# Moving the layer norms' subtraction and multiplication from VectorE to GpSimd in a two-layer cross-attention block

## The chip, the cores and the metric

The kernel runs on one core of one Trainium2 chip. The metric is the device time of one execution in microseconds. Engines are named as the profile names them: PE (TensorE matmul), PEld (TensorE weight load), DVE (VectorE), ACT (ScalarE), POOL (GpSimd) and SP (SyncE, which here issues nearly all DMAs).

## The reference

Two transformer layers run on `x` of 4 x 512 x 320 floats with a context of 4 x 1601 x 192. Each layer has three blocks, and each block begins with a layer norm over the 320 features:

```python
def _ln(x, g, b):
    m = jnp.mean(x, axis=-1, keepdims=True)
    v = jnp.mean(jnp.square(x - m), axis=-1, keepdims=True)
    return (x - m) * jax.lax.rsqrt(v + EPS) * g + b
...
h1 = _ln(x, n1_g, n1_b)
x = _attn(h1, h1, q1, k1, v1, o1_w, o1_b, heads) + x        # 20 heads of 16
h2 = _ln(x, n2_g, n2_b)
x = _attn(h2, context, q2, k2, v2, o2_w, o2_b, heads) + x   # keys and values from the context
h3 = _ln(x, n3_g, n3_b)
proj = h3 @ ff_w1 + ff_b1
a, g = jnp.split(proj, 2, axis=-1)
return a * jax.nn.gelu(g, approximate=False) @ ff_w2 + ff_b2 + x
```

So there are 2 layers x 3 blocks x 4 batches = 24 norms, each over 512 rows, which lie as four tiles of 128 rows by 320 features.

## The kernel before

**Units.** The work is cut into 88 units in a fixed order. In each layer come 20 self-attention units (4 batches x 5 groups of 4 heads), then 20 cross-attention units in the same way, then 4 feed-forward units. An attention unit goes over its keys in chunks of 128: 4 chunks in self attention, 13 in cross attention. For each chunk PE makes the scores of four heads (`st`, line 1282), ACT takes the exponential into a buffer `pr` (line 1292), and PE multiplies with the values (`av`, line 1308). ACT copies the product out of PSUM (`vo`, line 1327) and POOL adds it to the running sum `o` (line 1328). The pool `prs` has nine buffers for `pr` and `vo`.

**The work laid beside it.** The row maxima that the softmax of a coming unit needs are made early. PE makes score products into PSUM banks (`sps`, line 1054) while the current unit runs, and DVE reduces each bank to a maximum (`pm` or `nmax`, line 1069). There are eight PSUM banks for everything, so a bank that DVE has not read yet holds PE up. At the end of that, `max_end` turns the maxima, and four DMAs on SP's queue bring them to the rows that the scores need (`nrows<-turned`, line 1133). After a unit, `oway<-o` (line 1152) sends the sums to DRAM, on SP's queue too.

**Rounds and chains.** While the program is written, a counter `clock["round"]` is stepped twice a chunk. All other work (projections, norms, values, divisions, context) stands in chains: `add(chain, cost, f, due, ready, soon)` appends a step, and `steps()` runs, after each round of products, those heads of chains whose conditions hold, the earliest due first, as the credit allows. A step with cost `LIGHT` also uses up one of the one or two lights of that call; a step with cost 0.0 does not. On each engine instructions run in the order written.

**A norm** is `add_norm(l, b, i, ...)`: `i` is 0 for self attention, 1 for cross attention, 2 for feed forward. `stats` takes mean and variance of each tile on DVE (lines 546 and 547), `root` finds the reciprocal square root by Newton steps, on POOL after the start (lines 513 and 520 to 523). Then there are two ways:

- Norms with `first` (self attention of layer 0, self attention of batches 2 and 3 in layer 1, cross attention of batch 0) use `plain`: per tile three DVE instructions (line 608) subtract the mean, multiply, and write `hturned` with a step of 4 or 3 elements. Then `turn` transposes on PE (`hps`, line 621) and ACT applies gain and bias (line 629).
- The others use `normalise` (one DVE instruction per tile, line 562, into `hn`, which has one buffer) and `blocks` (a DVE transpose of 32 x 32 blocks into `hturned`, line 568). Then DMAs on SP's queue bring the blocks into place (line 578), and POOL applies gain and bias (`affine`, line 595).

The norm of a batch runs while earlier units still compute; `until_normed` would force what is left of it when a unit needs it.

Of the kernel before, what the change touches and what calls it, by code (L numbers as in the profile page):

```python
# [24 lines left out]
NQ = N // P  # L25
# [50 lines left out]
def kernel(ctx: ExitStack, tc: tile.TileContext, x, context, ws, out):  # L76
# [18 lines left out]
    nc = tc.nc  # L95
# [199 lines left out]
    class Unit:  # L295


        def __init__(self, l, kind, b, g):
            self.l, self.kind, self.b, self.g = l, kind, b, g
            self.cross = kind == "cross"  # L300
            self.nkeys = S2 if self.cross else N
            self.nch = (self.nkeys + P - 1) // P

            self.moves = {"k": deque(), "q": deque()}
            self.moving = {"k": 0, "q": 0}
            self.open = 6 if self.cross else 3
            self.keyed = None
            self.when = None
            self.vmade = [0, 0]

            self.made = {"q": 0, "k": 0, "kv": 0}
            self.scored = 0
            self.valued = 0
            self.steps = 2 * self.nch if kind != "ff" else 2 * NHC + NQ
            self.before = None
            self.others = []
            self.early = False
            self.own = {}
            self.pairs = self.hT = self.kvT = None
# [63 lines left out]
    clock = {"round": 0, "credit": 0.0, "lights": 0, "tiles": None, "ff": False}  # L383
    ALIKE = ("project", "early", "proj", "values")
    LIGHT = 0.01
# [3 lines left out]
    start = {"on": True}  # L389
# [22 lines left out]
    def busy(engine, us, *tiles):  # L412
        expect[engine] = max([expect[engine]] + [bank_of[id(t)][3] + 0.05 for t in tiles]) + us
        for t in tiles:
            bank_free[bank_of[id(t)][0]] = expect[engine] + 0.09
# [12 lines left out]
    def add(chain, cost, f, due, ready=yes, soon=yes):  # L428
        chains[chain].append((cost if isinstance(cost, tuple) else (cost,), due, ready, soon, f))
# [74 lines left out]
    def guess_root(var):  # L504

        a, h, y, z = (two.tile([P, NQ], F32, tag=f"root{i}", name=f"root{i}") for i in range(4))
        nc.vector.tensor_scalar(a, var, EPS, None, ALU.add)
        nc.vector.tensor_scalar(
            z.bitcast(I32), a.bitcast(I32), 1, None, ALU.logical_shift_right
        )  # L510
        nc.vector.tensor_scalar(y.bitcast(I32), z.bitcast(I32), -1, 0x5F3759DF, ALU.mult, ALU.add)
        eng = nc.vector if start["on"] else nc.gpsimd
        eng.tensor_scalar(h, a, -0.5, None, ALU.mult)
        return h, y, z

    def better_root(h, y, z):


        eng = nc.vector if start["on"] else nc.gpsimd
        eng.tensor_tensor(z, y, y, ALU.mult)  # L520
        eng.tensor_tensor(z, z, h, ALU.mult)
        eng.tensor_scalar(z, z, 1.5, None, ALU.add)
        eng.tensor_tensor(y, y, z, ALU.mult)
# [13 lines left out]
    def add_norm(l, b, i, put, done, due):  # L537
        xb = xs[b]
        s = {}

        def stats(t):
            if t == 0:
                hn_used.append(b)
                s["mv"] = two.tile([P, NQ, 2], F32, tag="mv", name="mv")
            st = three.tile([P, 6], F32, tag="st6", name="st6")
            nc.vector.bn_stats(st, xb[:, t, :])
            nc.vector.bn_aggr(s["mv"][:, t, :], st)
            busy("dve", 0.65)

        def root(step):  # L550
            if step == 0:
                s["root"] = guess_root(s["mv"][:, :, 1])
                s["rstd"] = s["root"][1]
            for _ in range(step + 1):
                better_root(*s["root"])
            s["round"] = clock["round"]

        def normalise(t):
            if t == 0:
                s["turned"] = one.tile([P, DB, NQ, SLOT], F32, tag="hturned", name="hturned")  # L560
            s["hn"] = one.tile([P, D], F32, tag="hn", name="hn")
            nc.vector.tensor_scalar(
                s["hn"], xb[:, t, :], s["mv"][:, t, 0:1], s["rstd"][:, t : t + 1], ALU.subtract, ALU.mult,
            )
            busy("dve", 0.4)

        def blocks(t):
            nc.vector.transpose(s["turned"][:, :, t, :], s["hn"])
            busy("dve", 0.45)
            s["round"] = clock["round"]  # L570
# [32 lines left out]
        def plain(t):  # L603
            if t == 0:
                s["hn"] = one.tile([P, DB, NQ, SLOT], F32, tag="hturned", name="hturned").rearrange("p k t w -> p (k t w)")
            for k, at, n in HK:
                w = n // SLOT
                nc.vector.tensor_scalar(  # L608
                    s["hn"][:, t * D + at : t * D + at + n].rearrange("p (d k) -> p k d", k=w),
                    xb[:, t, at : at + n].rearrange("p (k d) -> p k d", k=w),  # L610
                    s["mv"][:, t, 0:1], s["rstd"][:, t : t + 1], ALU.subtract, ALU.mult,
                )
            busy("dve", 0.45)
            s["round"] = clock["round"]

        def turn(k, at, n):
# [19 lines left out]
        first = i == 0 and (l == 0 or b > 1) or i == 1 and b == 0  # L636
        ahead = 0 if first or i == 2 and b else EARLIER
        parts = [(0, 0, P, 0), (1, 4, 96, 0), (2, 7, 96, 0)]
        if i == 2:
            parts = [(0, 0, P, 0), (1, 4, P, 0), (2, 8, REST, 0), (2, 8, REST, REST)]  # L640
        left, moved = [len(parts) * P // SLOT], {}

        def later(n, key="round"):
            return lambda: clock["round"] >= s[key] + n

        def together(f):
            return [lambda ts=ts: [f(t) for t in ts] for ts in (((0, 1), (2, 3)) if i == 2 and b else ((0,), (1,), (2,), (3,)))]

        for t, f in enumerate(together(stats)):
            add(  # L650
                "norm", LIGHT, f, due - ahead - 22 + t,
                (lambda: stage[b] == 3 * l + i and not hn_used and b in loaded) if t == 0 else yes,
                (lambda: b == 0 or clock["round"] >= loaded[b] + 5) if t == 0 else yes,
            )
        for step in range(2):
            add(
                "norm", 0.0 if step else LIGHT, lambda step=step: root(step), due - ahead - 18 + step, yes,
                (lambda: clock["round"] > s["round"]) if step else yes,
            )
        if first:  # L660
            for t in range(NQ):
                add("norm", LIGHT, lambda t=t: plain(t), due - 13 + t, yes, yes if t else later(1))
            for k, at, n in HK:
                add(
                    "norm", 0.58, lambda k=k, at=at, n=n: turn(k, at, n), due - 6 + 2 * k,
                    may_overwrite if k == 0 else yes, later(1),
                )
            return
        for t, f in enumerate(together(lambda t: (normalise(t), blocks(t)))):
            add("norm", LIGHT, f, due - ahead - 13 + t, yes, yes if t else later(1))  # L670
        add("norm", 0.0, spread, due - ahead - 6, may_overwrite, later(1))

        def there(k):
# [106 lines left out]
    errands = deque()  # L780
# [333 lines left out]
    def max_end(u):  # L1114

        top, high, low = (u.nm[:, :, i, :] for i in range(3))
        nc.vector.tensor_reduce(
            high.bitcast(F32R), top.rearrange("p j (t o) -> p j t o", o=1), AX.X, ALU.max, negate=True
        )
        nc.vector.tensor_reduce(  # L1120
            low, u.nm[:, :, 0:2, :].rearrange("p j e t -> p j t e"), AX.X, ALU.add, negate=True
        )
        turned = two.tile([P, SLOT], F32, tag="turned", name="turned")

        nc.vector.transpose(turned.rearrange("p (j c) -> p j c", j=HG), u.nm[:, :, 1:3, :].rearrange("p j e t -> p j (e t)"))
        busy("dve", 0.6)
        slots = u.rows.bitcast(F32).rearrange("(g s) n -> s g n", s=DH)[0].rearrange("g (t r) -> g t r", t=NQ)

        def rows():
            for i in range(P // SLOT):  # L1130
                part = slice(i * SLOT, (i + 1) * SLOT)
                queue = (nc.sync, nc.scalar, nc.gpsimd, nc.sync)[i] if start["on"] else nc.sync
                queue.dma_start(out=slots[:, :, part], in_=turned[part, :])

        if u.cross and u.before.cross:
            errands.appendleft((clock["round"] + 1, yes, rows))
        else:
            rows()
# [133 lines left out]
    def main(u, give, nxt):  # L1272

        pr, raised = {}, {}

        def score(c, j):
            r = min(P, u.nkeys - c * P)
# [383 lines left out]
    first = units[0]  # L1661
# [69 lines left out]
```

## Time and profile before

| what | value |
|---|---|
| median of 3 runs | 2983.01 us (2982.85 to 2983.1) |
| profiled execution, own time | 2982.2 us |
| its span | 2980.4 us |
| mean granted PE clock | 0.994 |
| PE busy | 2874.4 us (96%) |
| DVE busy | 2119.6 us (71%) |
| ACT busy | 1889.8 us (63%) |
| POOL busy | 1193.4 us (40%) |

The page gives busy time by engine, the chain of work that ended last, and groups of instructions by line. A group's row has the engine, what it writes and reads, the shapes, the count, the busy sum, the mean duration in ns, and what the engine waited for before. Lines in these rows are those of the kernel before. The table of stretches gives, for each stretch of the span, the busy time of each engine with the number of instructions in brackets.

### The profile page before, as it was taken

To read this page: it belongs to the slowest core of one execution; us is meant where nothing else is said; L and a number is where in the kernel's file an instruction comes from. 1 tells how busy PE (TensorE), PEld (TensorE's weight loads), DVE (VectorE), ACT (ScalarE), POOL (GpSimd) and SP (SyncE) were. 2 spreads that over 40 slices of the span, in tenths; PEclk is the share of its full clock that TensorE was granted. 3 is DMA by queue.
4 is the path that set the end of the run, shared out by engine and by line. 5 is a ranking of instruction groups with operands and counts; after the bars stand their busy time and mean duration, and the time that the engine had idled before them with its cause. 6 is when DMAs were issued, how large, how long until landed. Compare 5 with 4: busy or idle time off the path is not lost.

```text
span 2980.4 us, 84363 instructions
## 1 busy us (share of the span) xinstructions
PE 2874.4 (96%) x35018; PEld 1511.5 (51%) x35018; DVE 2119.6 (71%) x4143; ACT 1889.8 (63%) x3746; POOL 1193.4 (40%) x1305
## 2 busy tenths in 40 slices
PE   8999999999999999999999899999999999999999
PEld 4455555555554555355554555555555555544555
DVE  7877888889889888323268778888898888873221
ACT  3766677877877878501137676778878778784000
POOL 3445344554544545211224443445445454451110
PEclk8999999999999999999999999999999999999999
DMA  4443233132132122200123342221221121222000
GB/s 105 104 125 97 71 80 95 49 89 60 48 91 68 39 56 61 83 17 14 38 60 73 92 100 68 61 61 48 62 64 46 49 71 42 55 56 77 23 22 14
DMA packets 186543, 188.70 MB, mean 63 GB/s; under 512 B 69668, under 2 KB 137264, under 8 KB 186160
## 3 DMA queue, kind: packets, MB, share of 16 engines
q1 hardware_dynamic: 185368, 182.11, 24.2%
q8 instruction: 276, 4.52, 0.6%
q10 hardware_dynamic: 760, 1.18, 0.2%
q14 instruction: 107, 0.88, 0.1%
q0 software_dynamic: 32, 0.00, 0.0%
HBM read 55.76 MB, written 29.36 MB: 29 GB/s over the span
## 4 chain that ended last, share of the span: by engine, by line
PE 79%; DVE 16%; ACT 1%; DMA 1%; issue 1%; POOL 1%; SPq 0%; ACTq 0%; POOLq 0%; DVEq 0%
PE av L1308 22%; PE st L1282 16%; PE fps L1393 9%; DVE pm L1069 8%; PE sps L1054 6%; PE yps L1500 6%; PE vps L1015 5%; DVE nmax L1069 4%; PE kps L951 4%; PE ops L1211 3%; PE qkps L886 3%; PE fps L1453 2%; PE qps L927 2%; PE sps L1081 1%; ACT pr L1292 1%; DVE hturned L608 1%
## 5 line engine op out<-in xcount | busy, mean ns | idle before, releaser
L1292 ACT ACTIVATE pr<-st 128x512 f32<-128x512 f32 (+1 forms) x2720 | 1405.1, 603 | 418.3 <-PE st L1282 382.4
L1069 DVE TENSOR_REDUCE pm<-sps 128x1 f32<-128x512 f32 x1920 | 1187.2, 682 | 136.3 <-PE sps L1054 125.8
L1328 POOL TENSOR_TENSOR o<-o,vo 128x512 f32<-128x512 f32 x576 | 740.3, 1285 | 1101.8 <-ACT vo L1327 1091.9
L1054 PE MATMUL sps<-kT,q 32*128 32x512 f32 x4800 | 866.5, 429 | 12.2 <-DMA q<-low 3.2
L1308 PE MATMUL av<-pr,vals 128*32 128x512 f32 (+1 forms) x5440 | 735.1, 606 | 72.3 <-DVE nmax L1069 18.5
L1282 PE MATMUL st<-q,kT 32*128 32x512 f32 (+1 forms) x5120 | 791.6, 421 | 1.3 <-DVE pm L1069 0.8
L1282 PEld LDWEIGHTS st<-q,kT 32*128 32x128 f32 (+1 forms) x5120 | 420.7, 180 | 289.7 <-issue 119.1
L1282 PE MATMUL st<-nrows,ones 32*128 32x512 f32 (+1 forms) x2720 | 542.5, 400 | 8.5 <-DMA nrows<-turned 8.5
L1054 PEld LDWEIGHTS sps<-kT,q 32*128 32x128 f32 x4800 | 423.4, 184 | 93.3 <-DVE nmax L1069 15.7
L1069 DVE TENSOR_REDUCE nmax<-sps 128x1 f32<-128x512 f32 x640 | 395.7, 681 | 85.9 <-PE sps L1054 83.0
L1327 ACT COPY vo<-av 128x512 f32<-128x512 f32 x576 | 352.4, 612 | 20.9 <-PE av L1308 19.9
L1464 ACT ACTIVATE gl<-fps,b 128x512 f32<-128x512 f32 x80 | 54.8, 687 | 414.3 <-PE fps L1453 303.0
L1308 PEld LDWEIGHTS av<-pr,vals 128*32 128x32 f32 (+1 forms) x5440 | 111.1, 108 | 347.2 <-DVE pm L1069 179.4
L1393 PE MATMUL fps<-hT,w 128*128 128x512 f32 x640 | 283.2, 597 | 0.0
L1282 PEld LDWEIGHTS st<-nrows,ones 32*128 32x128 f32 (+1 forms) x2720 | 246.7, 180 | 33.2 <-issue 7.2
L1465 DVE SCALAR_TENSOR_TENSOR hid<-fps,b,gl 128x512 f32<-128x512 f32 x80 | 59.7, 748 | 238.8 <-ACT gl L1464 236.7
L1393 PEld LDWEIGHTS fps<-hT,w 128*128 128x128 f32 x640 | 119.2, 190 | 155.1 <-issue 151.8
L1500 PE MATMUL yps<-w,hid 128*128 128x320 f32 x640 | 176.0, 435 | 0.1
L1500 PEld LDWEIGHTS yps<-w,hid 128*128 128x128 f32 x640 | 120.4, 190 | 56.5 <-ACT gl L1464 5.3
L1211 PEld LDWEIGHTS ops<-wo,aT 112*32 112x32 f32 (+1 forms) x3072 | 97.7, 110 | 64.1 <-issue 42.9
L1211 PE MATMUL ops<-wo,aT 112*32 112x160 f32 (+1 forms) x3072 | 125.9, 300 | 0.9 <-DVE pm L1069 0.7
L886 PE MATMUL qkps<-hT,wqk 96*32 96x256 f32 (+1 forms) x1920 | 121.3, 395 | 0.0
(89 smaller groups left out, 2340.2 us busy)
## 6 DMA issues: line engine op xcount, KB each, us to landing
kT<-stages SPq DMA_DIRECT2D x160, 200.2 KB
oway<-o SPq DMA_DIRECT2D x80, 256.0 KB
q<-high SPq DMA_DIRECT2D x160, 64.0 KB
q<-low SPq DMA_DIRECT2D x160, 64.0 KB
kT<-high SPq DMA_DIRECT2D x60, 128.0 KB
q<-high SPq DMA_DIRECT2D x60, 128.0 KB
kT<-low SPq DMA_DIRECT2D x57, 128.0 KB
aT<-oway SPq DMA_DIRECT2D x32, 224.0 KB
```

The costliest lines, as they stand in the source:

```text
L886: nc.tensor.matmul(ps[f : f + m, :w], lhsT=wqk[:n, k, f // GD, column : column + m], rhs=first.hT[:n, k, at : at + w], start=(k == 0), sto ...
L1015: nc.tensor.matmul(ps[f : f + m, :w], lhsT=u.kvT[:n, k, at + f : at + f + m], rhs=wv[:n, k, h0 * DH : h1 * DH], start=(k == 0), stop=(k == ...
L1054: nc.tensor.matmul(ps, lhsT=u.q[j * SLOT : (j + 1) * SLOT, e, t * P : (t + 1) * P], rhs=u.kT[j * SLOT : (j + 1) * SLOT, u.k0 + s * 512 : u ...
L1069: nc.vector.tensor_reduce(to[:, j : j + 1], ps, AX.X, ALU.max)
L1211: nc.tensor.matmul(ps[f : f + m, : D // 2], lhsT=aT[:n, k, f * NQ + t * SLOT : f * NQ + t * SLOT + m], rhs=wo[:n, k, cols], start=(k == 0) ...
L1282: nc.tensor.matmul(own[0][:r, :], lhsT=ones[rows, :r] if e == 2 else u.keys(rows, c), rhs=u.rows[rows, :] if e == 2 else u.q[rows, e, :], ...
L1292: nc.scalar.activation(p[:r], own[0][:r], AF.Exp)
L1308: nc.tensor.matmul(ps[j * SLOT : (j + 1) * SLOT, :], lhsT=columns_of[:r, head : head + SLOT], rhs=pr.pop((c, j))[:r, :], start=True, stop= ...
L1327: nc.scalar.copy(vo, ps)
L1328: nc.gpsimd.tensor_tensor(u.o, u.o, vo, ALU.add)
L1393: nc.tensor.matmul(ps, lhsT=w1[:, k, i * FF + c * P : i * FF + (c + 1) * P], rhs=natural(u.hT[:, k]), start=start, stop=stop,)
L1500: nc.tensor.matmul(ps[:, :D], lhsT=hid[c][:, t * P : (t + 1) * P], rhs=w2[:, c, :], start=(c == 0), stop=(c == NHC - 1),)
```

## The change

The subtraction and multiplication of a norm go from DVE to POOL in three places: in `plain` whenever the kernel is past its start, and in `normalise` unless the norm is `alone`, that is self attention (`i == 0`) or feed forward of batches 1 to 3. So it moves `normalise` of cross attention in batches 1 to 3 and of feed forward in batch 0, and `plain` of all its norms but the first two, which are run at the start. The model of engine times that the planner keeps (`busy("dve", ...)`) is told of DVE work only where DVE still does it. The moved steps cost 0.0 and no light.

The order in time is set anew around them. `first` norms past the start begin four rounds sooner (`sooner`), their tiles are at least one round apart, and the PE transposes follow four rounds after the last tile instead of one. In the other moved norms, `normalise` of a tile and its `blocks` are now steps of their own, at least two rounds apart, with due times three rounds apart from tile to tile.

The last edit runs, at the start of a cross unit's `main`, the four row DMAs of that unit if they still stand in `errands`.

```diff
@@ add_norm
+        alone = i == 2 and b > 0 or i == 0
...
-            nc.vector.tensor_scalar(
+            (nc.vector if alone else nc.gpsimd).tensor_scalar(
                 s["hn"], xb[:, t, :], s["mv"][:, t, 0:1], s["rstd"][:, t : t + 1], ALU.subtract, ALU.mult,
             )
-            busy("dve", 0.4)
+            if alone:
+                busy("dve", 0.4)
+            s["round"] = clock["round"]
...
-                nc.vector.tensor_scalar(
+                (nc.vector if start["on"] else nc.gpsimd).tensor_scalar(
                     s["hn"][:, t * D + at : t * D + at + n].rearrange("p (d k) -> p k d", k=w),
...
-            busy("dve", 0.45)
+            if start["on"]:
+                busy("dve", 0.45)
...
+        sooner = 4 if first and not start["on"] else 0
...
-                "norm", LIGHT, f, due - ahead - 22 + t,
+                "norm", LIGHT, f, due - ahead - 22 - sooner + t,
...
-                "norm", 0.0 if step else LIGHT, lambda step=step: root(step), due - ahead - 18 + step, yes,
+                "norm", 0.0 if step else LIGHT, lambda step=step: root(step), due - ahead - 18 - sooner + step, yes,
...
-                add("norm", LIGHT, lambda t=t: plain(t), due - 13 + t, yes, yes if t else later(1))
+                add("norm", LIGHT if start["on"] else 0.0, lambda t=t: plain(t), due - 13 - sooner + t, yes, later(1))
...
-                    may_overwrite if k == 0 else yes, later(1),
+                    may_overwrite if k == 0 else yes, later(1 if k or start["on"] else 4),
...
-        for t, f in enumerate(together(lambda t: (normalise(t), blocks(t)))):
-            add("norm", LIGHT, f, due - ahead - 13 + t, yes, yes if t else later(1))
+        if alone:
+            for t, f in enumerate(together(lambda t: (normalise(t), blocks(t)))):
+                add("norm", LIGHT, f, due - ahead - 13 + t, yes, yes if t else later(1))
+        else:
+            for t in range(NQ):
+                add("norm", 0.0, lambda t=t: normalise(t), due - ahead - 17 + 3 * t, yes, later(1))
+                add("norm", LIGHT, lambda t=t: blocks(t), due - ahead - 15 + 3 * t, yes, later(2))
@@ max_end
         if u.cross and u.before.cross:
+            u.rows_of = rows
             errands.appendleft((clock["round"] + 1, yes, rows))
@@ main
+        for todo in [e for e in errands if e[2] is u.rows_of]:
+            errands.remove(todo)
+            todo[2]()
```

More of the change, by code (lines that the diff above doesn't have):

```diff
@@ L300, in __init__ @@
             self.cross = kind == "cross"
+            self.rows_of = None
             self.nkeys = S2 if self.cross else N
```

## The prediction

> **What bounds the kernel now.** I read the page's engine table first, then the chain that ended last, then the rows of the norm, then tables of stretches around the norms.
>
> ```profile
> span 2980.4 us, 84363 instructions
> PE 2874.4 (96%) x35018; PEld 1511.5 (51%) x35018; DVE 2119.6 (71%) x4143; ACT 1889.8 (63%) x3746; POOL 1193.4 (40%) x1305
> ...
> PE 79%; DVE 16%; ACT 1%; DMA 1%; issue 1%; POOL 1%; SPq 0%; ACTq 0%; POOLq 0%; DVEq 0%
> ```
>
> PE is busy for 96% of the span, so PE's work is the floor, and what can be won is time in which PE waits: 2980.4 - 2874.4 = 106 us idle, plus whatever waiting hides inside modelled matmul ends. The chain says who makes PE wait: 16% of it runs over DVE, nearly nothing over POOL. POOL has 60% of the span free. So a DVE instruction that stands ahead of the maxima can cost time, and the same instruction on POOL is at first sight free. The question is how much of the moved work stands where PE waits. One stretch of self attention, as the chain in order of time, shows it:
>
> ```profile
> by line: DVE nmax L1069 45.7%; DVE hturned L608 29.5%; PE av L1308 13.2%; PE qkps L886 8.1%; PE st L1282 4.1%; issue 0.6%; PE sps L1054 0.4%
> ...
> 99.11 2.48 DVE nmax L1069 x4
> 101.60 2.34 DVE hturned L608 x6
> 103.94 0.58 DVE nmax L1069
> ```
>
> Two tiles of `plain` (six instructions, 2.34 us) stand in DVE's queue between the maxima; PE's next products wait until DVE has read the banks. That is the best case for the change. The next rows are what is moved and what it could cost on POOL.
>
> ```profile
> L562 DVE TENSOR_SCALAR hn<-x,mv,root 128x320 f32<-128x320 f32 x64 | 41.9, 654 | 9.2 <-POOL root L523 8.1
> L608 DVE TENSOR_SCALAR hturned<-x,mv,root 128x96 f32<-128x96 f32 x64 | 21.6, 393 | 0.0
> L595 POOL TENSOR_SCALAR hT<-hT,lng,lnb 128x512 f32<-128x512 f32 x32 | 24.7, 772 | 127.6 <-DMA hT<-hturned 116.0 <-PE ops L1211 11.6
> L522 POOL TENSOR_SCALAR root<-root 128x4 f32<-128x4 f32 x66 | 14.8, 224 | 5.8
> ...
> L507 DVE TENSOR_SCALAR root<-mv x24: 157/170/1068, 5.8 to 2866.0; 128x4 f32<-128x4 f32 x24
> ```
>
> **What leaves DVE.** Six norms lose `plain` (24 tiles, 72 instructions) and eight lose `normalise` (32 instructions). The busy time of just those, by stretches that hold them and no others, and of the transposes that stay beside the 32:
>
> ```profile
> 60.00:360.00 300.00, 15.60 (x36) 1.00 0.40 102
> 1530.00:1750.00 220.00, 14.79 (x36) 0.97 0.36 88
> ...
> sum 1340.00, DVE 27.13; mean DVE 13.57
> ...
> sum 1340.00, DVE 16.36; mean DVE 8.18
> ```
>
> The first two rows are line 608 in the two self stages (15.60 + 14.79 = 30.4 us), the third is line 562 in cross attention (27.1 us), the last is line 568 there (16.4 us). So 57.5 us leave DVE, but most of a DVE microsecond is not a PE microsecond. I size that by PE's idle time in the stretches with a moved norm, against stretches of equal length right behind them. Columns after the length: PE, PEld, DVE, ACT, POOL busy. First self attention, with `plain`, then the stretches behind:
>
> ```profile
> 98.00:114.00 16.00, 13.32 (x194) 6.76 (x184) 15.13 (x32) 11.19 (x23) 7.27 (x13) 1.00 0.40 94
> ...
> 1575.00:1593.00 18.00, 13.87 (x180) 7.12 (x180) 14.45 (x30) 11.26 (x23) 7.44 (x15) 0.91 0.22 51
> 1655.00:1673.00 18.00, 12.64 (x164) 5.96 (x160) 13.12 (x29) 10.03 (x21) 7.62 (x15) 0.91 0.44 116
> ...
> sum 94.00, PE 75.85 PEld 38.91 DVE 84.41 ACT 61.90 POOL 43.27; mean PE 12.64 PEld 6.48 DVE 14.07 ACT 10.32 POOL 7.21
> ```
> ```profile
> sum 94.00, PE 91.97 PEld 50.36 DVE 67.31 ACT 73.33 POOL 36.83; mean PE 15.33 PEld 8.39 DVE 11.22 ACT 12.22 POOL 6.14
> ```
>
> With `plain`, DVE is busy for 84.41 of 94 us and PE idles 94 - 75.85 = 18.2 us; behind it PE idles 2.0 us. Two of the six stretches (1575 and 1655) hold 4.13 + 5.36 = 9.5 of that, with DVE far from full, so something other than DVE's load waits there. The other four idle (18.2 - 9.5) / 4 = 2.2 us each. I count all six at 2.2 and take the usual idle off: 6 x 2.2 - 2.0 = **11 us** from `plain`. Counting the two in full would give 16.
>
> Cross attention in the same way, eight stretches with `normalise` and eight behind:
>
> ```profile
> 702.00:720.00 18.00, 16.45 (x244) 8.11 (x240) 17.77 (x31) 13.47 (x27) 8.31 (x15) 1.00 0.51 132
> ...
> sum 122.00, PE 111.01 PEld 53.99 DVE 118.04 ACT 88.98 POOL 60.23; mean PE 13.88 PEld 6.75 DVE 14.75 ACT 11.12 POOL 7.53
> ```
> ```profile
> 720.00:738.00 18.00, 17.71 (x280) 10.23 (x284) 14.85 (x32) 13.35 (x28) 7.05 (x6) 1.00 0.16 34
> ...
> sum 122.00, PE 119.91 PEld 68.84 DVE 97.26 ACT 91.84 POOL 41.84; mean PE 14.99 PEld 8.60 DVE 12.16 ACT 11.48 POOL 5.23
> ```
>
> DVE is nearly full here (118.04 of 122), PE idles 11.0 us against 2.1 us, an excess of 8.9 us. The transposes stay, so I give the change the moved share of the norm's DVE time: 27.1 / (27.1 + 16.4) = 62% of 8.9 = **5.5 us**. All of it, if the transposes alone fit into DVE's slack, would be 8.9.
>
> Why `normalise` is as dear as 654 ns in the mean is seen in its spread and in the order of time:
>
> ```profile
> L562 DVE TENSOR_SCALAR hn<-x,mv,root x64: 426/446/1507, 496.7 to 2876.6; 128x320 f32<-128x320 f32 x64
> ```
> ```profile
> 704.64 1.29 POOL L1328 TENSOR_TENSOR o<-o,vo 128x512 f32<-128x512 f32 x1
> 704.84 1.27 DVE L562 TENSOR_SCALAR hn<-x,mv,root 128x320 f32<-128x320 f32 x1
> 706.15 0.51 DVE L568 STREAM_TRANSPOSE hturned<-hn 128x320 f32<-128x320 f32 x1
> 708.41 1.29 POOL L1328 TENSOR_TENSOR o<-o,vo 128x512 f32<-128x512 f32 x1 [2.48 <-ACT vo L1327]
> 708.95 0.93 DVE L562 TENSOR_SCALAR hn<-x,mv,root 128x320 f32<-128x320 f32 x1
> ```
>
> It takes 446 ns in the median, yet 1270 ns when it starts 0.2 us behind POOL's addition, and it then ends just behind that. The Trainium skill ("SBUF — State Buffer", section "SBUF: two separate sides") says that such a DVE operation and a GpSimd operation lock one port pair, and the later one waits for the whole of the other. The trace agrees. If the long ones were chance instead, 32 x 0.446 = 14.3 us would be what leaves, and the share would be 14.3 / (14.3 + 16.4) = 47%, so 4.2 us in place of 5.5.
>
> **What comes to POOL.** POOL's one-tensor rows give 224 ns for 4 elements and 772 for 512, so (772 - 224) / 508 = 1.08 ns an element. As estimates from these: `normalise` 224 + 316 x 1.08 = 0.57 us. `plain` writes with a step, which no POOL row shows; DVE's row does: (393 - 170) / 92 = 2.4 ns an element for 96 of them, taking line 507's median of 170 ns as fixed, against (446 - 170) / 316 = 0.87 without step (446 is line 562's median), a factor of 2.8. So a tile costs POOL between 1.0 us (no penalty) and 1.6 us (the same factor); I take 1.6, since the layout is the one that DVE pays for. POOL gains 24 x 1.6 + 32 x 0.57 = 57 us on 1193.
>
> In cross attention this is covered: the first addition above ends at 705.93, a `normalise` behind it at about 706.5, and its transpose, which now stands a chunk later on DVE, would come where `hn` started at 708.95. If that cover were gone, the transpose would hold the maxima behind it on DVE. The next `normalise` waits on POOL for that transpose, as `hn` has one buffer, and POOL's next addition stands behind it. In self attention the PE transposes come four rounds after the last tile, two chunks; the `LIGHT` steps beside them only gain lights. The DMAs `hT<-hturned` and the additions of a bias move later with the transposes; the due times begin 4 rounds earlier against that, so I cost it at nothing; if a unit had to wait for its norm, that would be one late tile, below. The edit in `main` issues the same four DMAs, at the latest where they are needed: nothing. For what the new order of the chains does to DMA landings I take one late tile, **+1.5 us**; its bounds I put at 5 us either way, about one wait of the size of `nrows` below.
>
> The sum: -11 - 5.5 + 1.5 = **-15 us**. The profiled execution took 2982.2 us (its span 2980.4), 0.8 us less than the median of the three runs, 2983.0. Against the median: **2968 us**. About 0.2% (6 us) is what a measurement of this kernel can tell from no change.
>
> **The rivals.**
>
> *More than that.* The stretches at 1575 and 1655 come back in full (16 in place of 11), and all of cross attention's excess (8.9), since the maxima also stop queueing behind port waits: -25, so about 2957 us, same verdict.
>
> *The maxima stay the limit.* In the chain of the stretch shown, `nmax` holds more than `hturned`. If DVE is full there anyway and only the order of its backlog changes, PE waits for the next maxima in place of the norm. Against it speaks that DVE drops to 67.31 of 94 us behind those stretches. It would leave what cross attention gives at most in its low case, 4 us, less the 1.5: about 2981 us. The same comes if the steps are put where DVE was idle.
>
> *GpSimd becomes the late one (slower).* POOL works in order, and SP too:
>
> ```profile
> SPq L1133 <- DVE turned L1125: 478.4, 61, 21.0
> SPq L1152 <- POOL o L1328: 257.8, 63, 9.1
> ...
> PE st L1282 <- DMA nrows<-turned: 8.5, 8, 2.4
> ...
> 1814.76 1.30 POOL o L1328
> 1816.06 0.02 issue
> 1816.08 7.36 DMA oway<-o
> 1823.44 0.02 issue
> 1823.46 4.31 DMA nrows<-turned
> ```
>
> SP waits 257.8 us in sum for POOL's `o`, and once already this ran on to PE: `o`, then `oway`, then `nrows` queued behind it. If `plain` ahead of `o` delays this by a part of its 1.6 us on each of 24 tiles, the gain of 15 is gone at 15 / 24 = 0.6 us a tile; with 1.0 us passed on it is 2983 - 15 + 24 = 2992 us. The chain's 1% for POOL speaks against it, and that PE waits for `nrows` 8 times in all, 8.5 us in sum. The Trainium skill ("GPSIMD Engine Reference", section 4.1) speaks for it: elementwise work is to stay on VectorE, GpSimd being about twice as slow for two inputs and about even for one. At twice DVE's 446 ns a `normalise` would be 0.89 us and not 0.57, which cross attention's cover above would still hold.
>
> **How the numbers follow.** Chances: the forecast 0.60; more than that 0.17; the maxima stay the limit 0.12; GpSimd late 0.11. Faster by over 0.2%: 0.60 + 0.17 = 0.77; within 0.2%: 0.12; slower: 0.11. The range goes from the larger gain with the new order's 5 us in its favour, 2957 - 5 = 2952, to 2988, which takes in the limit by maxima with those 5 us against it (2981 + 5) and the mild half of the late GpSimd; the rest of that, and gains beyond 25 us, are left out.
>
> **What would show it.** Right: DVE's busy time falls by some 55 us, and POOL's rises by 40 to 75; `hturned` of line 608 leaves the chain past the start; in the stretches of the moved norms PE idles 1 us each rather than 2.2. POOL's strided instructions tell the step's price: 0.5 to 0.6 us each, or 0.35 without. Wrong: DVE's transposes or PE's `hps` wait for POOL for more than a few us in sum, SP's wait for `o` grows by tens of us, or PE's waits for DVE only move to the next maxima.

## The result and the profile after

| | before | after |
|---|---|---|
| median | 2982.93 us (2981.72 to 2983.1) | 2954.43 us (2949.73 to 2956.35) |
| profiled execution, own time | 2982.2 us | 2956.35 us |
| its span | 2980.4 us | 2954.6 us |

The changed kernel is faster by 28.5 us: the ratio of times is 0.9905, with a 95% interval of 0.9891 to 0.9919. The forecast was 15 us, with the right sign and half the size.

The page after, its engine table and the chain by engine:

```profile
span 2954.6 us, 84378 instructions
PE 2872.8 (97%) x35018; PEld 1514.5 (51%) x35018; DVE 2060.8 (70%) x4031; ACT 1890.9 (64%) x3754; POOL 1290.0 (44%) x1409
...
PE 81%; DVE 13%; DMA 2%; ACT 1%; SPq 1%; issue 1%; POOL 1%; ACTq 0%; POOLq 0%; DVEq 0%
```

PE's work is the same (2872.8 us busy against 2874.4), and its idle time fell from 106 to 2954.6 - 2872.8 = 82 us. So 24 of the 25.8 us between the spans are waits that went. DVE is busy for 58.8 us less, as forecast (55). POOL is busy for 96.6 us more, where 40 to 75 was forecast. The groups show why: POOL's moved instructions (the three rows of POOL) take far longer than was worked out from its other rows. Lines are now those of the changed kernel: 564 is `normalise`, 612 `plain`, 572 the transpose of `blocks`.

```profile
L564 POOL TENSOR_SCALAR hn<-x,mv,root 128x320 f32<-128x320 f32 x32 | 46.1, 1440 | 0.0
...
L612 POOL TENSOR_SCALAR hturned<-x,mv,root 128x96 f32<-128x96 f32 x48 | 34.0, 744 | 0.0
...
L572 DVE STREAM_TRANSPOSE hturned<-hn 128x320 f32<-128x320 f32 x64 | 32.5, 508 | 4.9 <-POOL hn L564 3.8
...
L612 POOL TENSOR_SCALAR hturned<-x,mv,root 128x128 f32<-128x128 f32 x24 | 22.4, 933 | 0.0
```

Where the time went by stage is not in one view. I counted ACT's exponentials (16 in a self unit, 52 in a cross unit): the last of a stage's exponentials marks its end, and for feed forward the last write of `x`. The table has the change of each stage's length against the profiled execution of before, in us; the kernels below the first are those of the experiments. Each row is one execution, and executions of one kernel lie up to 12 us apart (`order_only`), so a difference of a few us between two rows proves little by itself.

| kernel | self 0 | cross 0 | self 1 | cross 1 | all |
|---|---|---|---|---|---|
| after | -1.0 | -3.0 | -14.8 | -7.1 | -25.8 |
| order_only | +4.6 | +3.9 | -6.2 | -6.5 | -4.2 |
| engine_only | +2.8 | +21.3 | -2.5 | +24.0 | +45.7 |
| plain_only | -2.8 | +7.9 | -18.0 | +6.0 | -7.0 |
| norm_only | -2.1 | -1.4 | -1.9 | -4.4 | -9.8 |
| split_dve | -0.9 | +3.1 | -2.7 | -7.0 | -7.5 |
| norm_twice | -2.7 | +11.4 | -16.4 | +3.0 | -4.7 |
| pool_mult_add | +1.4 | -3.9 | -18.0 | -7.5 | -27.9 |
| rows_ctx | -1.5 | -5.5 | -15.8 | -7.4 | -30.2 |
| rows_cross | -2.2 | -6.9 | -14.4 | -7.4 | -30.9 |
| rows_cross_add | -2.7 | -9.9 | -18.1 | -7.3 | -38.0 |

The feed-forward stages differ by at most 0.1 us everywhere. The two layers do the same work, yet the first self stage gained 1 us and the second 15. That asymmetry is the first thing to explain, and a few large waits make it. In the kernel before, PE stands still at two norms of the second self stage, for 3.0 and 4.3 us; the columns of these stretches are PE, PEld, DVE, ACT and POOL busy, then the granted clock:

```profile
1579.50:1582.30 2.80, 0.00 (x0) 0.00 (x0) 2.80 (x7) 1.54 (x4) 0.82 (x1) 1.00 0.08 9
1658.00:1661.90 3.90, 0.00 (x0) 0.00 (x0) 3.08 (x7) 1.49 (x4) 1.83 (x4) 1.00 0.85 227
```
```profile
1583.60:1586.90 3.30, 3.30 (x36) 1.68 (x32) 1.04 (x4) 1.03 (x2) 0.00 (x0) 0.50 0.17 63
1662.10:1665.40 3.30, 3.28 (x24) 1.18 (x28) 2.23 (x6) 0.59 (x1) 0.00 (x0) 0.50 0.04 11
```

Right behind each of these waits PE runs at a granted clock of 0.50 for about 3.4 us, so a wait costs more than its own length. Both waits are gone after. But the changed kernel has two new ones in the first layer, of 1.9 and 3.0 us, with their own half clock behind them:

```profile
200.70:202.40 1.70, 0.00 (x0) 0.00 (x0) 1.02 (x2) 0.39 (x2) 0.00 (x0) 1.00 0.52 95
475.80:478.60 2.80, 0.00 (x0) 0.00 (x0) 1.29 (x2) 0.00 (x0) 0.19 (x1) 1.00 0.05 6
```
```profile
203.30:210.00 6.70, 6.56 (x65) 3.58 (x65) 1.61 (x3) 3.05 (x7) 2.77 (x3) 0.50 0.11 35
479.80:486.50 6.70, 6.70 (x52) 2.80 (x56) 4.58 (x9) 4.13 (x9) 1.27 (x1) 0.50 0.26 59
```

Here the half clock lasts 6.8 us, which costs at most half of that. So as an estimate the new waits cost at most 1.9 + 3.4 = 5.3 and 3.0 + 3.4 = 6.4 us, and every kernel below has its own set of them.

One more pair is nearly a draw. PE's wait of 2.4 us at 1825 us for `nrows` behind `oway`, whose chain the prediction showed, is gone, and one of the same kind has come, 2.1 us at 1644 us; each has 3.4 us of half clock behind it:

```profile
1634.34 7.34 DMA oway<-o
1641.70 4.22 DMA nrows<-turned
```

The chain of before shows what made the wait at 1579 us, and with it what the prediction had set aside:

```profile
1577.15 0.21 POOL root L521
...
1578.90 0.21 POOL root L523
1579.11 0.02 issue
1579.13 2.68 DVE hturned L608 x6
1581.81 0.58 DVE nmax L1069
```

DVE stood at `plain` until POOL had finished `root`, whose last eight instructions (two Newton steps of four) stand behind an addition of `o`; the maxima that PE needed were queued behind `plain`. It is not DVE's load that counts here but its place in the order: the instruction at its head waited for POOL.

### The profile page after: what moved, and what is told of

The parts are those of the page before. It is cut to its first block, busy times and chain, and to the rows that moved or that the text cites. A ratio compares the mean times of both kernels' runs of the same rounds, so it can differ in the third digit from the quotient of the medians.

```text
span 2954.6 us, 84378 instructions
## 1 busy us (share of the span) xinstructions
PE 2872.8 (97%) x35018; PEld 1514.5 (51%) x35018; DVE 2060.8 (70%) x4031; ACT 1890.9 (64%) x3754; POOL 1290.0 (44%) x1409
## 4 chain that ended last, share of the span: by engine, by line
PE 81%; DVE 13%; DMA 2%; ACT 1%; SPq 1%; issue 1%; POOL 1%; ACTq 0%; POOLq 0%; DVEq 0%
PE av L1323 22%; PE st L1297 16%; PE fps L1408 9%; DVE pm L1080 8%; PE sps L1065 6%; PE yps L1515 6%; PE vps L1026 5%; PE ops L1223 3%; PE kps L962 3%; PE qkps L897 3%; DVE nmax L1080 3%; PE fps L1468 2%; PE qps L938 2%; PE sps L1092 1%; ACT pr L1307 1%
## 5 line engine op out<-in xcount | busy, mean ns | idle before, releaser
L1343 POOL TENSOR_TENSOR o<-o,vo 128x512 f32<-128x512 f32 x576 | 740.2, 1285 | 966.7 <-ACT vo L1342 950.1
L1297 PE MATMUL st<-q,kT 32*128 32x512 f32 (+1 forms) x5120 | 782.9, 421 | 2.2 <-ACT low L913 1.9
```

Of the source, the lines that this page charges most:

```text
L1297: nc.tensor.matmul(own[0][:r, :], lhsT=ones[rows, :r] if e == 2 else u.keys(rows, c), rhs=u.rows[rows, :] if e == 2 else u.q[rows, e, :], ...
L1343: nc.gpsimd.tensor_tensor(u.o, u.o, vo, ALU.add)
```

## The experiments

Medians are compared with the kernel before that ran beside them (2981.9 us in the first four, 2982.9 in the others).

### Order and engine apart

`order_only` has the changed kernel's order with DVE doing the arithmetic; PE, ACT and SP have the same instructions in the same order as in the changed kernel.

```diff
-                (nc.vector if start["on"] else nc.gpsimd).tensor_scalar(
+                nc.vector.tensor_scalar(                                   # plain
-            (nc.vector if alone else nc.gpsimd).tensor_scalar(
+            nc.vector.tensor_scalar(                                       # normalise
```

> The new order with all of the norm's arithmetic back on DVE: every instruction stands where the changed kernel has it, only the engine of the 104 moved ones is the old one. Relief theory (the gain is the 57 us that leave DVE): most of the gain is gone, 2975 to 2990 us. Order theory (the gain of 28.5 us is the new order, which by chance avoids the waits at 1579, 1658 and 1825 us of the kernel before): 2953 to 2965 us.

Measured: 2975.6 us, ratio 0.9976 (0.9966 to 0.9986), so 6.3 us faster than before and 21 us slower than the changed kernel. This is at the lower edge of what the relief theory gave, and excludes the order theory's 2953 to 2965. In its self stages the waits of before are still there, and PE is idle:

```profile
1587.60:1590.00 2.40, 0.00 (x0) 0.00 (x0) 1.98 (x5) 0.81 (x2) 1.51 (x3) 1.00 0.01 2
1663.90:1667.30 3.40, 0.00 (x0) 0.00 (x0) 1.99 (x5) 0.72 (x2) 2.23 (x6) 1.00 0.79 228
```

The chain ahead of the first again runs over POOL's `root` into DVE's `plain`. So the new order alone does not remove these two waits; in that order, moving `plain` to the engine that also makes `root` does. In the self stages the engine is worth (4.6 + 1.0) + (14.8 - 6.2) = 14.2 us in one and the same order. In the cross stages it is (3.9 + 3.0) + (7.1 - 6.5) = 7.5 us, nearly all of it in the first layer, where `order_only` has larger waits of its own (3.8 us at 481 us, with 10 us at half clock, and 1.5 us at 1082 us, with 6.8 us).

`engine_only` is the other corner: before's order, with POOL doing the arithmetic.

```diff
-                nc.vector.tensor_scalar(                                   # plain, in the kernel before
+                (nc.vector if start["on"] else nc.gpsimd).tensor_scalar(
-            nc.vector.tensor_scalar(                                       # normalise
+            (nc.vector if i == 2 and b > 0 or i == 0 else nc.gpsimd).tensor_scalar(
```

> The order of the kernel before, with only the engine of the same 104 instructions changed to POOL. Relief theory: the plain part gains its 15 us or so; in the other part each DVE transpose now stands right behind a POOL instruction of 1.44 us and waits for it, which costs DVE what it saves, so 2962 to 2975 us, with tens of us of DVE transposes waiting for POOL. Order theory: no gain without the order, 2978 to 2995 us.

Measured: 3028.42 us, ratio 1.0151 (1.0133 to 1.0169): slower by 46.5 us, far outside both expectations. The self stages hardly changed (+2.8, -2.5); the cross stages lost 21 and 24 us. For these the waits tell it in one row (sum, times, longest):

```profile
DVE hturned L568 <- POOL hn L562: 70.0, 31, 5.3
```
```profile
L562 POOL TENSOR_SCALAR hn<-x,mv,root 128x320 f32<-128x320 f32 x32 | 46.0, 1436 | 4.9 <-DVE hturned L568 4.9
...
L568 DVE STREAM_TRANSPOSE hturned<-hn 128x320 f32<-128x320 f32 x64 | 32.7, 511 | 71.1 <-POOL hn L562 70.0
```

The transpose stands right behind `normalise` in the program. DVE waits there for POOL, 2.3 us in the mean, and the maxima wait behind it. I had counted only POOL's own 1.44 us; POOL also has the addition of `o` ahead of it, which waits for ACT. This is the rival "GpSimd becomes the late one", real and dear, but through DVE's queue and not through SP's. The change avoids it by its two rounds between `normalise` and `blocks`.

In the self stages the two waits of before are gone here too, but others stand in their place, of 1.3, 2.4 and 1.8 us at 1617, 1686 and 1762 us. The chain ahead of the first shows `plain` on POOL holding up the addition of `o`, and through it ACT, whose `hT` PE needs:

```profile
1612.58 4.34 POOL hturned L608 x6
1616.92 1.20 POOL o L1328
1618.12 0.02 issue
1618.14 0.58 ACT vo L1327
1618.73 1.35 ACT hT L629 x2
```

So neither half of the change explains the gain: the order alone gave 6 us, the engine alone lost 46, and both together gain 28.5. The engine's 14.2 us in the self stages exist only in the new order.

### One half at a time

```diff
+        alone = True                                   # plain_only: normalise as before
```

> Only plain (self attention, and cross attention of batch 0) moves to POOL with its new due times; normalise and its transposes stay one DVE step as before. Relief theory by the units' ends (self stages gained 1 + 15 us, cross stages 2 + 7 us): 2964 to 2971 us. Order theory: anything between 2955 and 2990, not the sum of the parts.

```diff
-            if start["on"]:                            # norm_only: plain as before
-                busy("dve", 0.45)
+            busy("dve", 0.45)
...
-        sooner = 4 if first and not start["on"] else 0
+        sooner = 0
...                                                     # plain on DVE, its old cost and conditions
```

> Only normalise (cross attention of batches 1 to 3, first feed-forward batch) moves to POOL, split from its transposes; plain stays on DVE with its old due times. Relief theory: the rest of the gain, 5 to 14 us, so 2969 to 2978 us, and with plain_only the two gains add up to 28 us within 6. Order theory: no such sum.

Measured: `plain_only` 2975.19 us, ratio 0.9976 (0.9966 to 0.9985); `norm_only` 2971.1 us, ratio 0.9961 (0.9946 to 0.9976). That is 6.7 + 10.8 = 17.5 us, not 28 within 6, so the sum expected of the relief theory failed. The stage table says where. `plain_only` gained 20.8 us in the self stages, where it acts, more than the whole change does there, but lost 7.9 in the first cross stage, whose norms it leaves on DVE: its trace has PE idle for 3.5 us at 474 us, and behind it

```profile
476.60:486.70 10.10, 9.17 (x68) 4.01 (x72) 4.81 (x9) 4.72 (x10) 1.27 (x1) 0.50 0.25 60
```

10 us at half clock, which is at most 5 us more. The rest, 6.0 us lost in the second cross stage, is spread over several norms in steps of 1 to 4 us, and I have no single cause for it. `norm_only` gained 5.8 us in the cross stages; its other 4.0 us lie in self stages, in which nothing that it moves runs. There before's wait at 1825 us is gone (2.4 us and its half clock), as it is in `split_dve` below, so that is not POOL's work. So other places of the schedule give and take as much as the halves themselves, and the two medians can't be added up.

### Is it the time or the place? Normalise on DVE, but apart from its transpose

`split_dve` is `norm_only` with `normalise` on DVE; PE, ACT and SP are in the same order.

```diff
-            (nc.vector if alone else nc.gpsimd).tensor_scalar(
+            nc.vector.tensor_scalar(                   # normalise, still two rounds ahead of blocks
```

> The order of norm_only (normalise split from its transpose by two rounds), with normalise on DVE: PE, ACT and SP stand exactly as in norm_only, only the engine of 32 instructions differs. Spacing theory (in cross attention the gain comes from cutting one DVE burst of about 1.4 us into two that are two rounds apart, as the cross stages of order_only hint): within 4 us of norm_only's 2971 us. Relief theory (the DVE time itself is what PE waits for): 5 to 11 us slower than norm_only, so 2976 to 2982 us.

Measured: 2975.24 us, ratio 0.9974 (0.9964 to 0.9983), 4.1 us slower than `norm_only` and 7.6 faster than before. That lies between the two theories, and the intervals of `split_dve` and `norm_only` overlap. So most of what `norm_only` gained, 7.6 of 10.8 us by the medians, came without any change of engine; in the cross stages of the traces it is 3.9 of 5.8 us. In the second cross stage `split_dve` gained 7.0 us where the changed kernel gained 7.1. Why the new place helps has at least two answers, which these runs do not part: one DVE burst is cut into two that are two rounds apart, and `normalise` stands less often behind an addition of POOL:

```profile
L564 DVE TENSOR_SCALAR hn<-x,mv,root 128x320 f32<-128x320 f32 x64 | 32.7, 511 | 9.6 <-POOL root L524 8.7
```

It takes 511 ns in the mean, against 654 before. All of that comes from the 32 that the change would move: 18.0 us in sum here, against 27.1 before. So 9 us of DVE's time went by place alone.

The edit in `main` has no part in the changed kernel's gain, as it never acts there: no cross unit starts with its row DMAs still in `errands`. In `norm_only` and `split_dve` one unit does.

### How much cover the two rounds give

`norm_twice` does POOL's `normalise` twice.

```diff
+            for _ in range(1 if alone else 2):
                 (nc.vector if alone else nc.gpsimd).tensor_scalar(
```

> The changed kernel with each of the 32 normalise on POOL done twice (2 x 1.44 us, same values). Cover theory (the transpose two rounds later comes well after POOL, as the prediction had it): 2954 to 2958 us. No-cover theory (in the changed kernel most transposes start 0.03 us after POOL's normalise ends): each of about 28 transposes waits up to 1.44 us more and holds the maxima behind it, so +10 to +35 us, 2964 to 2990 us.

Measured: 2975.29 us, ratio 0.9972 (0.9962 to 0.9983), so 21 us slower than the changed kernel. DVE waits for POOL at every one of the 32:

```profile
DVE hturned L573 <- POOL hn L565: 39.7, 32, 4.0
```

There is hardly any cover beyond what the change uses: 18 of the 32 transposes of the changed kernel start within 0.1 us of POOL's end, the others 0.1 to 0.9 us behind it. In the order of time, POOL and then DVE:

```profile
499.92 1.45 POOL L564 TENSOR_SCALAR hn<-x,mv,root 128x320 f32<-128x320 f32 x1
```
```profile
501.40 0.51 DVE L572 STREAM_TRANSPOSE hturned<-hn 128x320 f32<-128x320 f32 x1
```

499.92 + 1.45 = 501.37, and the transpose begins at 501.40.

### Why normalise takes 1.44 us on POOL

`pool_mult_add` leaves everything in its place and changes the two operations of the moved instructions. It no longer computes the norm, but x times the mean plus the reciprocal deviation.

```diff
-                s["hn"], xb[:, t, :], s["mv"][:, t, 0:1], s["rstd"][:, t : t + 1], ALU.subtract, ALU.mult,
+                ..., ALU.subtract if alone else ALU.mult, ALU.mult if alone else ALU.add,
```

> The changed kernel with the pair of operations that POOL does in the moved instructions set to multiply, add in place of subtract, multiply: it computes x*mean + rstd there, so the result is not the reference's; shapes, places and order are the same. If the pair of operations is what makes normalise take 1.44 us (the affine step's multiply, add takes 0.77 us for 512 elements): 0.57 us in the mean and plain at 0.35 to 0.6 us an instruction; the whole kernel then gains only what transposes wait for POOL now, 0 to 8 us: 2946 to 2955 us. If the tensor or its scalars are the cause: durations as before, and 2950 to 2957 us.

```profile
L612 POOL TENSOR_SCALAR hturned<-x,mv,root 128x96 f32<-128x96 f32 x48 | 21.2, 477 | 0.0
...
L564 POOL TENSOR_SCALAR hn<-x,mv,root 128x320 f32<-128x320 f32 x32 | 19.6, 611 | 0.0
...
L612 POOL TENSOR_SCALAR hturned<-x,mv,root 128x128 f32<-128x128 f32 x24 | 14.1, 588 | 0.0
```

The pair of operations is the cause: 611 ns in place of 1440 for the same tensors and scalars, and `plain` 477 and 588 in place of 744 and 933. Those are the prediction's estimates (0.57 us; 0.5 to 0.6). The kernel's time is 2953.0 us, ratio 0.9893 (0.9877 to 0.991), not to be told from the changed kernel's 2954.4. The cover explains that: here the transposes start 0.9 us behind POOL's end in the median, at the same distance of about 1.5 us from POOL's start as in the changed kernel. They go when DVE's queue comes to them, so a faster `normalise` finds little left to save.

### The two new waits

At 475.8 us PE waits for the row DMAs of the next unit. SP's queue there, in the changed kernel:

```profile
469.84 3.03 SPq L218 DMA_DIRECT2D lng<-in_L_xattn_n_g_dram  x3
472.92 1.89 SPq L218 DMA_DIRECT2D lnb<-in_L_xattn_n_b_dram  x3
474.90 2.67 SPq L1144 DMA_DIRECT2D nrows<-turned  x4
```

`turned` was ready at 469.1, but six loads for the next layer stood ahead of the four row DMAs. `rows_ctx` keeps loads out of that chunk and spreads the first context load, whose eight DMAs stand ahead of the wait at 200.7:

```diff
-            if loads:
+            if loads and (last or c != u.nch - 3):
                 loads.popleft()()
...
-            add("context", 0.0, ..., free if k == 0 else yes, later(2) if k else yes)
+            add("context", 0.0, ..., free if k == 0 else yes, later(4) if k else yes)
```

> The changed kernel with two edits of SP's queue alone: no loads of weights are issued in the chunk in which the next unit's row DMAs become ready, and the second half of the first context load comes four rounds after the first instead of two. PE, ACT, DVE and POOL stand as in the changed kernel. If the two new waits in layer 0 (PE idle at 200.6 and 475.7 us, each followed by 6.8 us at half clock) come from queueing on SP: 5 to 12 us faster than the changed kernel, 2942 to 2949 us. If they come from the moved work itself: no change, 2950 to 2957 us.

Measured: 2952.26 us, ratio 0.9893 (0.9879 to 0.9908). In its trace the wait at 475.8 is gone (the first cross stage gained 2.5 us more), but the one at 200 stays (PE idle for 1.6 us), PE waits 2.1 us at 117, since the edit also moved loads of self attention, and a gap of 1.5 us at 1066 is followed by half clock. At 200 us ACT waits for `q<-low`, and the run does not settle the part of the context load in that: the four DMAs that come later now stand between the DMAs of `q`, and that `q<-low` is issued behind them.

```profile
196.96 2.61 SPq L766 DMA_DIRECT2D w<-ctxT  x4
199.61 0.60 SPq L863 DMA_DIRECT2D q<-high  x1
200.25 0.59 SPq L863 DMA_DIRECT2D q<-low  x1
```

Why it lands late stays open.

`rows_cross` limits the edit to cross attention; only SP's queue differs from the changed kernel.

```diff
-            if loads:
+            if loads and not (u.cross and not last and c == u.nch - 3):
                 loads.popleft()()
```

> The changed kernel with one edit of SP's queue: in cross attention no loads of weights are issued in the chunk in which the next unit's row DMAs become ready. All other engines stand as in the changed kernel. If the wait at 475.7 us there is the row DMAs' place behind six loads on SP, and its length counts with the half clock behind it: PE's 3.0 us gap and the 6.8 us at half clock go, 4 to 7 us faster than the changed kernel, 2947 to 2951 us. If another wait takes their place: 2952 to 2957 us.

Measured: 2948.98 us, ratio 0.9884 (0.9869 to 0.9898), 5.4 us less than the changed kernel's median, as expected. Its interval and the changed kernel's overlap, so the size is loose; that the wait goes is seen in the trace. SP's queue:

```profile
468.54 2.67 SPq L1144 DMA_DIRECT2D nrows<-turned  x4
471.26 1.94 SPq L218 DMA_DIRECT2D lng<-in_L_xattn_n_g_dram  x3
```

The rows now go 6.4 us sooner, and neither the gap nor the half clock behind it is there. The first cross stage is 3.9 us shorter than the changed kernel's, although it has a new gap of 1.6 us at 1065 us with 3.4 us of half clock.

`rows_cross_add` adds the fast pair of operations in a form that computes the norm: x times the reciprocal deviation, plus an offset made once a norm.

```diff
+            if step and not start["on"] and not alone:
+                s["off"] = two.tile([P, NQ], F32, tag="off", name="off")
+                nc.gpsimd.tensor_tensor(s["off"], s["mv"][:, :, 0], s["rstd"], ALU.mult)
+                nc.gpsimd.tensor_scalar(s["off"], s["off"], -1.0, None, ALU.mult)
...
+                nc.gpsimd.tensor_scalar(..., s["rstd"][:, t : t + 1], s["off"][:, t : t + 1], ALU.mult, ALU.add)
```

> rows_cross with the moved instructions as multiply, add on POOL, with -mean/deviation made once a norm by two small POOL operations, so that it computes the reference. Normalise at about 0.6 us in place of 1.44, plain at about 0.5 in place of 0.75. Cover theory (POOL's part is off the path once the transposes stand two rounds later): the same as rows_cross within 4 us. If transposes now lose time to POOL: 4 to 10 us faster than rows_cross.

Measured: 2947.37 us, ratio 0.9884 (0.9867 to 0.99): the same as `rows_cross` within the spread, as the cover theory had it. By its median it is the fastest of all, 35.5 us below the kernel before and 7.1 below the changed one.

## Why the prediction was right, and only half in size

The measured 2954.4 us lie 2.4 us inside the lower end of the range. The direction and the place of the gain were right; both terms of the gain were too small.

- **What bounds the kernel.** Right: PE's work stayed, its waits fell by 24 us.
- **The 11 us of `plain`.** Mis-sized: the self stages gained 15.8 us net of new waits, 18.0 + 2.8 in `plain_only`. The failing step is "something other than DVE's load waits there", by which the stretches at 1575 and 1655 were cut from 9.5 us to 4.4. It was not load, but it was still the norm: DVE's `plain` waited for POOL's `root`. `order_only`, with `plain` on DVE, keeps both waits; with `plain` on POOL in the same order they are gone. They also cost more than PE's idle time, as half clock follows each; the two rows with a clock of 0.91 showed that, and I did not read them. Counting them in full, as the first rival did, gave 16.
- **The 5.5 us of `normalise`.** Mis-sized, and its mechanism half wrong. The cross stages gained 10.1 us, and 14.3 in `rows_cross`, without the wait at 475.8. The share by DVE time assumed that only time which leaves DVE helps, and that the transposes' part of PE's idle time stays. `split_dve` gained 3.9 us of `norm_only`'s 5.8 in these stages with the engine as it was: the new place alone shortened `normalise` and parted it from its transpose.
- **The cover.** Wrong in both its numbers, right in its verdict by luck. `normalise` was put at 0.57 us and is 1.44, since POOL's price hangs on the pair of operations; and the 2.4 us behind it were 0.9 in the median, as `pool_mult_add` shows, where POOL takes 0.61. The 0.9 us that were missed in the one are about the 0.9 us that there were in the other; `norm_twice` pays 21 us for twice the work. The factor of about two that the Trainium skill ("GPSIMD Engine Reference", section 4.1) gives for two inputs, and that gave 0.89 us, was too mild as well: against DVE's 446 ns the measured ratio is 3.2.
- **The port.** The Trainium skill's lock ("SBUF — State Buffer", "SBUF: two separate sides") still fits: POOL's additions kept their 1285 ns, and `normalise` on DVE fell from 654 to 511 ns where it stood elsewhere. What it alone is worth was not separated.
- **One late tile, 1.5 us.** Too small: the new order brought two waits in layer 0, and the kernel without one of them is 5.4 us faster by its median. The wait at 200 us has no cause that a run shows.
- **The rivals.** "More than that" (2957) is what came, and in its sizes too: 15.8 us where it had 16, and 10.1 where it had 8.9. Its first reason is shown; its second, the port waits, was not separated. The late GpSimd is what `engine_only` shows, 46 us, at a place where I had put the point of decision at 0.6 us a tile on another queue. That the maxima stay the limit did not happen.
- **The other signs.** They came out mild: in the changed kernel DVE's transposes wait 3.8 us in sum for POOL's `normalise`, PE's `hps` less than 2 us for POOL, and SP's wait for `o` grew by 10 us, from 257.8 to 267.8, where tens were to speak against the forecast.

## What to carry to other kernels

When an instruction leaves a busy engine, ask first what waits at its head, not how long it runs: an instruction that waits for a slower engine holds everything queued behind it. The same move changed the time by -28 us with its consumer two rounds later and by +46 us with the consumer right behind, so the distance is part of the change. Test the order and the engine apart: here neither was worth much without the other. And in a schedule full of short waits, look at the stage lengths and the granted clock before adding up medians of half changes; the four row DMAs issued 6 us sooner were worth some 4 to 5 us.

## What the runs showed of the hardware

- On POOL the pair subtract, multiply took 1440 ns for 128x320 floats, and multiply, add 611 ns, with tensors and scalars alike.
- `normalise` on DVE took 27.1 us for the 32 instructions of the kernel before that the change moves, and 18.0 us for the same 32 in `split_dve`, where they stand at other places between POOL's additions.
- PE waits of 1.2 to 4.3 us were often followed by 3.4, 6.8 or 10.2 us at a granted clock of 0.50. Past the first 90 us, the twelve traces have 82 such waits, and 51 of them had half clock within 4 us: 35 of the 43 above 2 us, 16 of the 39 below. The shortest was 1.2 us; one of 3.2 us in `engine_only` (2441 us) had none. The Trainium skill ("TensorE: Matmul & The Clock Gate", Part 1) has a free-running window of 3413 ns and half rate after an idle window. The lengths agree with whole windows. Its rule of thumb, no idle gaps over some 3.4 us, does not: gaps half as long were often enough here.
